# MLP, shared experts and router in an order written by hand on three engines, and slots' rows and gates loaded with their tokens

## The chip, the core and the metric

The kernel runs on one core of a Trainium2 chip. The metric is the device time of one execution in microseconds; the time before is the median of three runs. The core has a matrix engine (TensorE, PE in the profile), a vector engine (VectorE, DVE), a scalar engine (ScalarE, ACT), a general engine (GpSimd, POOL) and a synchronisation engine (SyncE, SP). Each works through its own list of instructions in order. Transfers between the chip's memory (HBM) and the on-chip buffers are issued from the lists of SyncE, ScalarE or GpSimd, and an issue that must wait holds what stands behind it in that list. A matmul writes to a bank of the accumulator memory, from which VectorE and ScalarE read.

## What is computed

One layer: 512 query rows of width 512 attend to 8192 context rows (16 heads), then a state-space block with a gated MLP, then a mixture of experts with top-2 routing and a shared expert. The reference, cut to what this change touches:

```python
x = x + _L0_xattn_ref(_layernorm(x), ctx, ctx, ...)          # cross attention
# state-space block and MLP, on the LayerNorm of x
z = layernorm(x)
z = z + _ssm(rmsnorm(z, norm1_w), ...)
h = rmsnorm(z, norm2_w)
mlp = (silu(h @ w1) * (h @ w3)) @ w2                          # D_FF = 2048
x = x + z + mlp
# experts, on the LayerNorm of x
t = layernorm(x)
logits = t @ router_w.T                                       # 16 experts
top_vals, top_idx = top_k(logits, 2)
gates = sigmoid(top_vals)
h_e = silu(t @ gate_e) * (t @ up_e)                           # EXPERT_DIM = 512
moe = sum over the two chosen experts of gate * (h_e @ down_e)
shared = (silu(t @ rsg.T) * (t @ rsu.T)) @ rsd.T              # SHARED_DIM = 1024
x = x + moe + shared
```

## The kernel before

Every f32 product is made of three f16 products (high times high, high times low, low times high), so a 128x128 by 256 block of the MLP costs three matmuls, and each f16 operand is a pair (high, low): ScalarE makes the high half by a cast or copy, VectorE the low half by a subtraction.

**Stages.** Attention over the context takes about the first two thirds. Then come the output projection, the state-space scan, the MLP, the LayerNorm `ln2`, the router, the shared experts and the experts. The 512 tokens are two halves s = 0, 1 of H = 256. The MLP of half 0 runs as filling inside the scan of half 1; the MLP of half 1, both halves of the shared experts and the router follow after the scan, and it is these that the change edits.

**`ffn` (L962-986)** is used for the MLP (weights w1, w3, w2; eight chunks f2) and for the shared experts (rsg, rsu, rsd; four chunks). For one chunk it loads three weight tiles `wpm` (ring of five slots, 512 KB each, from SyncE), runs 24 matmuls of 256 columns into the bank `pg` and 24 into `pu`, then g = silu(pg) on ScalarE (L973), g = pu * g on VectorE (L974), `gg` high half by a cast on ScalarE (L976), low half on VectorE (L977), and then 12 matmuls of 512 columns, `mm_down` (L716 to L718), into two accumulators. Banks pg, pu, and the banks of transposes and logits rotate over three. At its end the half's accumulators are added to `x_sb` (L985). It is a generator that yields once a chunk and is stepped by its callers.

**`ln2(s)` (L995-1019)** computes the statistics of x_sb (VectorE), a reciprocal root by Ln and Exp on ScalarE (L669, L670, each with a load of its activation table) and four small steps on VectorE, then the normalised tokens into `u_sb`, their transposes on TensorE, and the router's logits `plg` (24 small matmuls) copied to `lg`.

**Router (L1133-1215).** Tokens are written as f16 pairs to `xf`, whose rows have XR = 1028 16-bit words: 1024 for the pair, two for the token's row number, two for its gate. Then maxima and indices, sigmoid of the two best logits, ranks of tokens within experts by small matmuls (`prk`), slot numbers `sg` (L1191), and eight indirect DMAs from GpSimd (L1212), which scatter the rows to `xd_d` in HBM: four with the first gate, then, after a copy of the second gate into xf (L1210) that has to wait for the first four, four more. Slots are groups of 128 rows: one for each of the 16 experts and up to seven for overflow, two of which always run, so 18 slots k are processed. The overflow slots' expert numbers are put into `oii` (L1204), which SyncE reads into registers (L1342).

**Experts (L1217-1340).** `moe_load(k)` loads slot k with two DMAs that wait for all eight scatters: the token words `xd` from ScalarE's list (four buffers), and the last four words of the rows, `xm`, from GpSimd's list (eight buffers, 128 rows of 8 bytes). `moe_in` transposes xd to `xk`, `moe_up` makes 96 matmuls (banks pmg, pmu), `moe_mid` the activation, `moe_down` 12 matmuls, and `moe_out` scales with the gate on ScalarE (`myo`, L1284) and adds the rows to `sum_d` in HBM by an indirect, accumulating DMA from GpSimd (L1285). Each scatter-add waits for the one before it. Slots 0 to 2 are loaded ahead of the loop, slot k+3 within iteration k. Expert weights come as `piece`s of 512 KB (L1091-1106): a load into `wef` (six buffers, SyncE), a conversion to f16 on ScalarE (L1104) and its rest on VectorE (L1105). Twenty up-projection pieces (NWE) are made ahead of the experts.

**What sets the order.** All of this is written as source, but a scheduler places the instructions of each engine by its own costs, except within `manual_schedule`, where the named engines keep source order. Before, only the call of `moe` stands in such a block, with TensorE, VectorE and ScalarE named. So the twenty early pieces, which the source has last, are placed where the scheduler puts them: the profile has their conversions between 2249 and 2317. It also puts a part of each chunk's down matmuls inside the next chunk's gate block. SyncE's and GpSimd's lists are placed by the scheduler throughout. At the end the sum `sum_d` is started from x_sb by a DMA from GpSimd (L1347) and copied to the output (L1357).

## Time and profile before

| what | us |
|---|---|
| median of three runs | 2584.93 (2579.12 to 2588.01) |
| the profiled execution's own time | 2596.24 |
| its span, first to last instruction | 2594.4 |
| its mean granted TensorE clock | 0.973 of full speed |
| TensorE busy | 2376.9 (92%) |
| VectorE busy | 2045.9 (79%) |
| ScalarE busy | 1949.5 (75%) |
| GpSimd busy | 83.1 (3%) |
| first expert matmul (pmg) | 2407.5 |
| last scatter-add issued | 2581.8 |
| output copy issued | 2588.1 |

Times within the run are microseconds from the start of the span. In a listing by time a row is: start, duration, engine, line, operation, result <- operands, and in brackets the idle time of that engine before it and what ended it. In a list of waits a row is: engine, what waited and its line, what it waited for, the total in us, the number of times, and the longest. In a table of windows, each engine has its busy time and, in brackets, its number of instructions; the last three columns are the granted clock, the busy share of the DMA engines and the GB/s they moved. "L973" is line 973 of the kernel before. ACTq and SPq are the DMA issues of ScalarE and SyncE.

### The profile page before, as it was taken

What the parts mean: (1) busy time and instruction counts of PE and PEld (TensorE: products, weight loads), DVE (VectorE), ACT (ScalarE), POOL (GpSimd) and SP (SyncE); (2) the same over time, 40 slices, a digit from 0 to 9 for tenths busy, and PEclk for the clock granted to TensorE, in tenths of its full rate; (3) what the DMA queues carried; (4) which work ended last, traced back from release to release, by engine and by line L of the source; (5) the groups of instructions that cost most, each with busy time, mean ns of one, the idle gap of its engine ahead of it and who ended that gap; (6) DMA issues with size and microseconds to landing.
All of it is one profiled execution on the core that took longest, in us unless ns stands there. A gap on an engine that the chain in (4) does not pass through costs nothing. (4 is left out here: it accounts for less than half of the span.)

```text
span 2594.4 us, 56739 instructions
## 1 busy us (share of the span) xinstructions
PE 2376.9 (92%) x22958; PEld 1726.7 (67%) x22958; DVE 2045.9 (79%) x2378; ACT 1949.5 (75%) x3734; POOL 83.1 (3%) x92
## 2 busy tenths in 40 slices
PE   7999899999999999999999998998878687898996
PEld 3455577777677777666777776997656465665784
DVE  6776578888888888887888778997899999643684
ACT  5787788888788888878888887997868466432684
POOL 3000000000000000000000000000000000001122
PEclk9999999999999999999999999999989889999998
DMA  7883777788787787878787665888511222595796
GB/s 264 293 277 132 209 213 226 237 233 235 206 233 226 225 243 230 240 201 223 227 236 211 180 164 136 205 204 214 153 57 42 90 74 81 192 327 191 273 359 203
DMA packets 355967, 529.52 MB, mean 204 GB/s; under 512 B 28770, under 2 KB 222498, under 8 KB 355428
## 3 DMA queue, kind: packets, MB, share of 16 engines
q1 hardware_dynamic: 349156, 513.23, 65.7%
q0 software_dynamic: 3952, 7.89, 1.5%
q10 hardware_dynamic: 2592, 4.72, 0.5%
q8 instruction: 182, 2.98, 0.5%
q14 instruction: 85, 0.70, 0.1%
HBM read 396.65 MB, written 126.97 MB: 202 GB/s over the span
## 5 line engine op out<-in xcount | busy, mean ns | idle before, releaser
L380 DVE TENSOR_TENSOR phl<-p,phl 128x1024 f16<-128x1024 f32 x512 | 626.7, 1225 | 192.7 <-ACT phl L377 179.6
L375 ACT ACTIVATE p<-pss 128x512 f32<-128x512 f32 x1024 | 597.5, 622 | 113.6 <-issue 43.6
L308 ACT ACTIVATE sf<-psx 128x512 f16<-128x512 f32 x1024 | 558.7, 625 | 70.3 <-PE psx L303 69.5
L367 PE MATMUL pss<-qhh,k 128*128 128x256 f16 x2048 | 480.8, 275 | 11.2 <-ACT phl L377 10.3
L368 PE MATMUL pss<-qlm,kb 128*128 128x256 f16 x2048 | 479.0, 274 | 0.7 <-DMA kb<-k_d 0.5
L316 DVE TENSOR_TENSOR runm<-runm,sf 128x2048 f16<-128x2048 f16 x240 | 292.3, 1219 | 51.1 <-ACT sf L308 50.9
L397 PE MATMUL po<-v,phl 128*128 128x130 f16 x4096 | 323.7, 221 | 3.9 <-DVE oq L410 3.4
L377 ACT ACTIVATE phl<-pss 128x512 f16<-128x512 f32 x512 | 312.8, 611 | 0.0
L397 PEld LDWEIGHTS <-phl 128*128 128x128 f16 x4096 | 271.7, 98 | 61.7 <-issue 15.3
L278 PE MATMUL psv<-wh_v,ctxc 128*128 128x256 f16 x1024 | 283.4, 277 | 7.3 <-ACT wh_v L179 3.2
L279 PE MATMUL psv<-wl_v,ctxc 128*128 128x256 f16 x1024 | 282.2, 276 | 1.2 <-DVE wl_v L180 1.2
L280 PE MATMUL psv<-wh_v,ctxc 128*128 128x256 f16 x1024 | 282.0, 275 | 0.0
L367 PEld LDWEIGHTS <-k 128*128 128x128 f16 x2048 | 201.0, 98 | 64.7 <-issue 19.1
L368 PEld LDWEIGHTS <-kb 128*128 128x128 f16 x2048 | 201.3, 98 | 50.5 <-issue 12.7
L303 PE MATMUL psx<-khl,qh 64*128 64x512 f16 x1024 | 209.1, 386 | 18.7 <-ACT sf L308 13.2
L929 PE MATMUL py<-hs,ident 128*128 128x256 f32 x512 | 142.7, 434 | 74.0 <-DVE hs L926 73.9
L400 PE MATMUL po<-v,phl 128*128 128x65 f16 x4096 | 208.5, 193 | 1.3 <-DVE phl L380 1.2
L254 PE MATMUL psk<-ctxc,wh_k 128*128 128x512 f16 x512 | 197.9, 386 | 10.9 <-ACT ctxc L237 9.1
L379 DVE CAST phl<-p 128x1024 f16<-128x1024 f32 x256 | 176.1, 688 | 32.3 <-ACT p L375 32.1
L255 PE MATMUL psk<-ctxc,wh_k 128*128 128x512 f16 x512 | 196.3, 383 | 0.7 <-DVE ctxc L238 0.7
L256 PE MATMUL psk<-ctxc,wl_k 128*128 128x512 f16 x512 | 196.3, 383 | 0.0
L929 PEld LDWEIGHTS py<-hs,ident 128*128 128x128 f32 x512 | 106.0, 215 | 106.5 <-DVE hs L926 87.9
(308 smaller groups left out, 3834.8 us busy)
## 6 DMA issues: line engine op xcount, KB each, us to landing
v<-v_d SPq DMA_DIRECT2D x128, 520.0 KB, 5.3
k<-k_d SPq DMA_DIRECT2D x256, 256.0 KB, 4.7
ctxc<-ctx_d SPq DMA_DIRECT2D x96, 512.0 KB, 5.8
wef<-in_gu_dram SPq DMA_DIRECT2D x72, 512.0 KB, 6.8
v_d<-vs SPq DMA_DIRECT2D x128, 260.0 KB, 4.1
k_d<-khl SPq DMA_DIRECT2D x128, 256.0 KB, 3.0
kb<-k_d SPq DMA_DIRECT2D x128, 256.0 KB, 5.3
wpm<-w_d SPq DMA_DIRECT2D x48, 512.0 KB, 4.2
```

Of the source, the lines that this page charges most:

```text
L278: nc.tensor.matmul(ps[:, t, :], lhsT=ct[i // 2][:, 0, i % 2, sl], rhs=wh[:, i, :], start=i == 0, stop=False)
L279: nc.tensor.matmul(ps[:, t, :], lhsT=ct[i // 2][:, 0, i % 2, sl], rhs=wl[:, i, :], start=False, stop=False)
L280: nc.tensor.matmul(ps[:, t, :], lhsT=ct[i // 2][:, 1, i % 2, sl], rhs=wh[:, i, :], start=False, stop=i == NC4 - 1)
L308: nc.scalar.activation(dst, ps, AF.Copy, scale=1.0 / (8.0 * WS))
L316: nc.vector.tensor_tensor(r, r, sf, ALU.max)
L367: nc.tensor.matmul(ps[:, hh], lhsT=k[:, hh, sl], rhs=qhh[:, hh, qs], start=True, stop=False)
L368: nc.tensor.matmul(ps[:, hh], lhsT=b[:, hh, sl], rhs=qlm[:, hh, qs], start=False, stop=True)
L375: nc.scalar.activation(p32[:, i], pss[i], AF.Exp, scale=sc)
L377: nc.scalar.activation(ph[:, i], pss[i], AF.Exp, scale=sc)
L380: nc.vector.tensor_tensor(pl, p32, ph, ALU.subtract)
L397: nc.tensor.matmul(o, lhsT=ph[:, i, hh, qs], rhs=vv, start=first, stop=False, **kw)
L929: nc.tensor.matmul(py[:, j, :], lhsT=ident, rhs=hs[:, n, 1:], start=k == 0, stop=False)
```

## The change

1. `ffn_ordered` takes the place of `ffn` for the MLP of half 1 and for the shared experts. It writes a chunk as pg, pu with silu, the down matmuls of the chunk before, then g and gg, with three yields a chunk.
2. `ln2` becomes a generator, and the router's code moves into a generator `route`; their steps are interleaved with the chunks by counters.
3. The twenty early pieces are made one by one between the steps by `early` (nine in the MLP of half 1, five and six in the two halves of the shared experts).
4. The block in which TensorE, VectorE and ScalarE keep source order is opened ahead of `outproj(1)` and closed after `moe`.
5. The addition of u_sb to x_sb for half 1 moves out of `outproj` to after the rest of half 0's MLP.
6. `moe_load(k, queue)` loads the whole row of 1028 words by one DMA into `xd` (six buffers); row numbers and gates are read from it, and xm is gone. Slots 0 to 2 are loaded from GpSimd's list, later ones from ScalarE's.

```diff
@@ outproj
-        nc.vector.tensor_add(x_sb[:, ts_, :], x_sb[:, ts_, :], u_sb[:, ts_, :])
+        if not s:
+            nc.vector.tensor_add(x_sb[:, ts_, :], x_sb[:, ts_, :], u_sb[:, ts_, :])
...
+    def ffn_ordered(s, h2, names, pm):
...
+        prev = None
+        for f2 in range(nf):
+            wg, wu, wd = (wload(n, f2) for n in names)
+            pg = bank_j([P, 2, H], F32, "pg")
+            for j in range(2):
+                mm_block(pg[:, j, :], wg, j, h2[:, 0], h2[:, 1])
+            yield
+            pu = bank_j([P, 2, H], F32, "pu")
+            for j in range(2):
+                mm_block(pu[:, j, :], wu, j, h2[:, 0], h2[:, 1])
+            g = F2.tile([P, 2, H], F32, name="g32", bufs=2)
+            nc.scalar.activation(g, pg, AF.Silu, scale=IW)
+            yield
+            if prev:
+                down(*prev)
+            nc.vector.scalar_tensor_tensor(g, pu, IW, g, ALU.mult, ALU.mult)
+            gg = F2.tile([P, 2, 2, H], F16, name="gg", bufs=2)
+            nc.scalar.copy(gg[:, 0], g)
+            nc.vector.tensor_tensor(gg[:, 1], g, gg[:, 0], ALU.subtract)
+            yield
+            prev = f2, gg, wd
+        down(*prev)
+        yield
...
+    mo = ExitStack()
+    mo.enter_context(tc.manual_schedule(engines={mybir.EngineType.PE, mybir.EngineType.DVE, mybir.EngineType.Activation}))
     outproj(1, yTs[-1], h2s[1], lambda: next(ml, None))
     for _ in ml:
         pass
+    nc.vector.tensor_add(x_sb[:, 2:4, :], x_sb[:, 2:4, :], u_sb[:, 2:4, :])
...
+    mlp1 = ffn_ordered(1, h2s[1], MLP, [acc(0), acc(1)])
+    xT0, xT1 = h2tile(), None
+    l0 = ln2(0, xT0)
+    pre = iter(range(NWE))
+
+    def early():
+        n = next(pre, None)
+        if n is not None:
+            piece(n // 4, "gu", n % 4)
+
+    for n, _ in enumerate(mlp1):
+        if n in (0, 5, 7, 9):
+            next(l0, None)
+        if n % 3 == 1:
+            early()
+    xT1 = h2tile()
+    l1, ro = ln2(1, xT1), route()
+    rs0 = ffn_ordered(0, xT0, RS, [acc(3), acc(3)])
+    next(l1)
+    for n, _ in enumerate(rs0):
+        if n in (4, 5, 7):
+            next(l1, None)
+        elif n > 7:
+            next(ro, None)
+        if n % 3 == 1:
+            early()
+    for n, _ in enumerate(ffn_ordered(1, xT1, RS, [acc(3), acc(3)])):
+        next(ro, None)
+        early()
+    for _ in ro:
         pass
...
-    def moe_load(k):
+    def moe_load(k, queue):
         if k > lastk[0]:
             return
-        xds[k] = g2.tile([P, 2 * DM], U16, name="xd", bufs=4)
-        meta[k] = g2.tile([P, 4], U16, name="xm", bufs=8)
-        for q, t, c in ((nc.scalar, xds[k], slice(0, 2 * DM)), (nc.gpsimd, meta[k], slice(2 * DM, XR))):
-            r = q.dma_start(t, xd_d[k * P : (k + 1) * P, c])
+        xds[k] = g2.tile([P, XR], U16, name="xd", bufs=6)
+        r = queue.dma_start(xds[k], xd_d[k * P : (k + 1) * P, :])
...
         for k in range(ks[0], ks[0] + 3):
-            moe_load(k)
+            moe_load(k, nc.gpsimd)
...
-            moe_load(k + 3)
+            moe_load(k + 3, nc.scalar)
...
-    for _ in rs0:
-        pass
-    for _ in ffn(1, xT1, RS, [acc(3), acc(3)]):
-        pass
     nc.gpsimd.dma_start(sum_d[0:NQ].rearrange("(p i) d -> p i d", i=4), x_sb)
-    for n in range(NWE):
-        piece(n // 4, "gu", n % 4)
-    with tc.manual_schedule(engines={mybir.EngineType.PE, mybir.EngineType.DVE, mybir.EngineType.Activation}):
-        moe(range(16 + MOV), NWE)
+    moe(range(16 + MOV), NWE)
+    mo.close()
```

`route` holds the router's code of L1133 to L1215 in the same order, except that the computation of oii is moved behind the scatters, with seven yields between its parts: before the low half of xf, before the sigmoid, two before the rank matmuls (`prk`), one after them, one after the scatters and one at its end.

More of the change, by code (lines that the diff above doesn't have):

```diff
@@ L986, in ffn, with down @@
         yield
+    def ffn_ordered(s, h2, names, pm):
+        nf = len(mlp_d[names[0]])
+        def down(f2, gg, wd):
+            for i in range(2):
+                sl = slice(i * P, (i + 1) * P)
+                for j in range(2):
+                    k = 2 * f2 + j
+                    mm_down(pm[i], gg[:, 0, j, sl], gg[:, 1, j, sl], wd, j, k == 0, k == 2 * nf - 1)
+        prev = None
[6 more added lines that the diff above has]
+            pu = bank_j([P, 2, H], F32, "pu")
+            for j in range(2):
+                mm_block(pu[:, j, :], wu, j, h2[:, 0], h2[:, 1])
[12 more added lines that the diff above has]
+        yield
+        for i in range(2):
+            nc.vector.scalar_tensor_tensor(x_sb[:, 2 * s + i], pm[i], IW, x_sb[:, 2 * s + i], ALU.mult, ALU.add)
+        yield
     rwf = T.tile([P, NC4, 16], F32, name="rwf")
@@ L993, in tail, with ln2 @@
     lg = T.tile([P, 4, 16], F32, name="lg")
-    def ln2(s, xT, fill=lambda: None):
+    def ln2(s, xT):
         ts_ = slice(2 * s, 2 * s + 2)
@@ L1005, in ln2 @@
             )
-        fill()
+        yield
         transposeT(h, xT[:, 0], xT[:, 1])
-        fill()
+        yield
         pl = bank_j([P, 2, 16], F32, "plg")
@@ L1018, in ln2 @@
                     n += 1
+        yield
         nc.scalar.activation(lg[:, ts_, :], pl, AF.Copy, scale=IW)
+        yield
     MLP, RS = ("w1", "w3", "w2"), ("rsg", "rsu", "rsd")
@@ L1122, in tail @@
     nc.gpsimd.memset(one16, 1.0)
-    mlp1 = ffn(1, h2s[1], MLP, [acc(0), acc(1)])
-    next(mlp1)
-    xT0 = h2tile()
-    ln2(0, xT0, lambda: next(mlp1))
-    for _ in mlp1:
-        pass
-    xT1 = h2tile()
-    rs0 = ffn(0, xT0, RS, [acc(3), acc(3)])
-    ln2(1, xT1, lambda: next(rs0, None))
-    xf = const.tile([P, 4, XR], U16, name="xf", tag="big16")
-    xv = xf[:, :, 0 : 2 * DM].bitcast(F16)
-    nc.scalar.copy(xv[:, :, 0:DM], u_sb)
-    nc.vector.tensor_tensor(xv[:, :, DM : 2 * DM], u_sb, xv[:, :, 0:DM], ALU.subtract)
@@ L1137, in tail @@
-    nc.gpsimd.iota(xf[:, :, 2 * DM : 2 * DM + 2].bitcast(I32), pattern=[[1, 4], [0, 1]], base=0, channel_multiplier=4)
-    mx = G.tile([P, 4, 8], F32, name="mx8")
-    ix = G.tile([P, 4, 8], U32, name="ix8")
-    for i in range(4):
-        nc.vector.max(mx[:, i, :], lg[:, i, :])
-        nc.vector.max_index(ix[:, i, :], mx[:, i, :], lg[:, i, :])
-    ef = G.tile([P, 4, 2], F32, name="ef")
-    nc.vector.tensor_copy(ef, ix[:, :, 0:2])
-    gt = G.tile([P, 4, 2], F32, name="gt")
-    nc.scalar.activation(gt, mx[:, :, 0:2], AF.Sigmoid)
@@ L1148, in tail @@
-    oh = G.tile([P, 2, 4, 16], F32, name="oh")
-    iob = io16.unsqueeze(1).to_broadcast((P, 4, 16))
-    for j in range(2):
-        nc.vector.tensor_tensor(
-            oh[:, j], iob, ef[:, :, j : j + 1].to_broadcast((P, 4, 16)), ALU.is_equal
-        )
-    oht = G.tile([P, 4, 16], F16, name="oht")
-    nc.vector.tensor_add(oht, oh[:, 0], oh[:, 1])
-    next(rs0, None)
-    prk = bank_j([P, 5, 16], F32, "prk")
-    for i in range(5):
-        n = min(i, 4)
-        if i < 4:
-            nc.tensor.matmul(prk[:, i, :], lhsT=lt, rhs=oht[:, i, :], start=True, stop=n == 0)
-        for k in range(n):
-            nc.tensor.matmul(
-                prk[:, i, :], lhsT=ones, rhs=oht[:, k, :], start=i == 4 and k == 0, stop=k == n - 1
-            )
@@ L1166, in tail @@
-    rk = G.tile([P, 5, 16], F32, name="rk")
-    nc.vector.tensor_copy(rk, prk)
-    ov = G.tile([P, 16], F32, name="ov")
-    nc.vector.tensor_scalar(ov, rk[:, 4, :], 128.0, None, ALU.is_gt)
-    for th in (256.0, 384.0):
-        nc.vector.scalar_tensor_tensor(ov, rk[:, 4, :], th, ov, ALU.is_gt, ALU.add)
-    inc = G.tile([P, 16], F32, name="inc")
-    nc.vector.tensor_tensor_scan(inc, one16, ov, 0.0, ALU.mult, ALU.add)
-    ahi = G.tile([P, 16], F32, name="ahi")
-    nc.vector.tensor_sub(ahi, inc, ov)
@@ L1176, in tail @@
-    nc.vector.tensor_sub(ahi, ahi, io16)
-    nc.vector.tensor_scalar(ahi, ahi, 128.0, 15.0 * P, ALU.mult, ALU.add)
-    sl3 = G.tile([P, 4, 16], F32, name="sl3")
-    nc.vector.tensor_scalar(sl3, rk[:, 0:4, :], 128.0, None, ALU.is_ge)
-    nc.vector.tensor_mul(sl3, sl3, ahi.unsqueeze(1).to_broadcast((P, 4, 16)))
-    nc.vector.tensor_add(sl3, sl3, rk[:, 0:4, :])
-    e128 = G.tile([P, 16], F32, name="e128")
-    nc.vector.tensor_scalar(e128, io16, 128.0, None, ALU.mult)
-    nc.vector.tensor_add(sl3, sl3, e128.unsqueeze(1).to_broadcast((P, 4, 16)))
@@ L1185, in tail @@
-    sf_ = G.tile([P, 2, 4], F32, name="slf")
-    tmp = G.tile([P, 2, 4, 16], F32, name="tmp")
-    for j in range(2):
-        nc.vector.tensor_mul(tmp[:, j], oh[:, j], sl3)
-        nc.vector.tensor_reduce(sf_[:, j], tmp[:, j], axis=AX.X, op=ALU.add)
-    sg = G.tile([P, 2, 4], U32, name="sg")
-    nc.vector.tensor_copy(sg, sf_)
-    ct = G.tile([P, NOV, 16], F32, name="ct")
-    nc.vector.tensor_tensor(
-        ct,
-        inc.unsqueeze(1).to_broadcast((P, NOV, 16)),
-        io16[:, 0:NOV].unsqueeze(2).to_broadcast((P, NOV, 16)),
-        ALU.is_le,
-    )
@@ L1199, in tail @@
-    oid = G.tile([P, NOV + 1], F32, name="oid")
-    nc.vector.tensor_reduce(oid[:, 0:NOV], ct, axis=AX.X, op=ALU.add)
-    nc.vector.tensor_scalar(oid[:, 0:NOV], oid[:, 0:NOV], 15.0, None, ALU.min)
-    nc.vector.tensor_copy(oid[:, NOV : NOV + 1], inc[:, 15:16])
-    oii = G.tile([P, NOV + 1], I32, name="oii")
-    nc.vector.tensor_copy(oii, oid)
-    sent = []
-    gs = G.tile([P, 4, 2], F32, name="gs")
-    nc.vector.tensor_scalar(gs, gt, IW, None, ALU.mult)
-    for j in range(2):
-        nc.gpsimd.tensor_copy(xf[:, :, XR - 2 : XR].bitcast(F32), gs[:, :, j : j + 1])
-        for i in range(4):
-            d = nc.gpsimd.indirect_dma_start(
-                out=xd_d[:], out_offset=bass.IndirectOffsetOnAxis(ap=sg[:, j, i : i + 1], axis=0),
-                in_=xf[:, i], in_offset=None,
-            )
-            for o in sent:
-                tc.declare_no_dep(d.ins, o.ins, reason="every slot is one token's: the rows differ")
-            sent.append(d)
@@ L1220, in moe_load, with route @@
-    def moe_load(k):
+    oii = G.tile([P, NOV + 1], I32, name="oii")
+    sent = []
+    def route():
+        xf = const.tile([P, 4, XR], U16, name="xf", tag="big16")
+        xv = xf[:, :, 0 : 2 * DM].bitcast(F16)
+        nc.scalar.copy(xv[:, :, 0:DM], u_sb)
+        yield
+        nc.vector.tensor_tensor(xv[:, :, DM : 2 * DM], u_sb, xv[:, :, 0:DM], ALU.subtract)
+        nc.gpsimd.iota(xf[:, :, 2 * DM : 2 * DM + 2].bitcast(I32), pattern=[[1, 4], [0, 1]], base=0, channel_multiplier=4)
+        mx = G.tile([P, 4, 8], F32, name="mx8")
+        ix = G.tile([P, 4, 8], U32, name="ix8")
+        for i in range(4):
+            nc.vector.max(mx[:, i, :], lg[:, i, :])
+            nc.vector.max_index(ix[:, i, :], mx[:, i, :], lg[:, i, :])
+        ef = G.tile([P, 4, 2], F32, name="ef")
+        nc.vector.tensor_copy(ef, ix[:, :, 0:2])
+        gt = G.tile([P, 4, 2], F32, name="gt")
+        yield
+        nc.scalar.activation(gt, mx[:, :, 0:2], AF.Sigmoid)
+        oh = G.tile([P, 2, 4, 16], F32, name="oh")
+        iob = io16.unsqueeze(1).to_broadcast((P, 4, 16))
+        for j in range(2):
+            nc.vector.tensor_tensor(
+                oh[:, j], iob, ef[:, :, j : j + 1].to_broadcast((P, 4, 16)), ALU.is_equal
+            )
+        oht = G.tile([P, 4, 16], F16, name="oht")
+        nc.vector.tensor_add(oht, oh[:, 0], oh[:, 1])
+        yield
+        yield
+        prk = bank_j([P, 5, 16], F32, "prk")
+        for i in range(5):
+            n = min(i, 4)
+            if i < 4:
+                nc.tensor.matmul(prk[:, i, :], lhsT=lt, rhs=oht[:, i, :], start=True, stop=n == 0)
+            for k in range(n):
+                nc.tensor.matmul(
+                    prk[:, i, :], lhsT=ones, rhs=oht[:, k, :], start=i == 4 and k == 0, stop=k == n - 1
+                )
+        yield
+        rk = G.tile([P, 5, 16], F32, name="rk")
+        nc.vector.tensor_copy(rk, prk)
+        ov = G.tile([P, 16], F32, name="ov")
+        nc.vector.tensor_scalar(ov, rk[:, 4, :], 128.0, None, ALU.is_gt)
+        for th in (256.0, 384.0):
+            nc.vector.scalar_tensor_tensor(ov, rk[:, 4, :], th, ov, ALU.is_gt, ALU.add)
+        inc = G.tile([P, 16], F32, name="inc")
+        nc.vector.tensor_tensor_scan(inc, one16, ov, 0.0, ALU.mult, ALU.add)
+        ahi = G.tile([P, 16], F32, name="ahi")
+        nc.vector.tensor_sub(ahi, inc, ov)
+        nc.vector.tensor_sub(ahi, ahi, io16)
+        nc.vector.tensor_scalar(ahi, ahi, 128.0, 15.0 * P, ALU.mult, ALU.add)
+        sl3 = G.tile([P, 4, 16], F32, name="sl3")
+        nc.vector.tensor_scalar(sl3, rk[:, 0:4, :], 128.0, None, ALU.is_ge)
+        nc.vector.tensor_mul(sl3, sl3, ahi.unsqueeze(1).to_broadcast((P, 4, 16)))
+        nc.vector.tensor_add(sl3, sl3, rk[:, 0:4, :])
+        e128 = G.tile([P, 16], F32, name="e128")
+        nc.vector.tensor_scalar(e128, io16, 128.0, None, ALU.mult)
+        nc.vector.tensor_add(sl3, sl3, e128.unsqueeze(1).to_broadcast((P, 4, 16)))
+        sf_ = G.tile([P, 2, 4], F32, name="slf")
+        tmp = G.tile([P, 2, 4, 16], F32, name="tmp")
+        for j in range(2):
+            nc.vector.tensor_mul(tmp[:, j], oh[:, j], sl3)
+            nc.vector.tensor_reduce(sf_[:, j], tmp[:, j], axis=AX.X, op=ALU.add)
+        sg = G.tile([P, 2, 4], U32, name="sg")
+        nc.vector.tensor_copy(sg, sf_)
+        gs = G.tile([P, 4, 2], F32, name="gs")
+        nc.vector.tensor_scalar(gs, gt, IW, None, ALU.mult)
+        for j in range(2):
+            nc.gpsimd.tensor_copy(xf[:, :, XR - 2 : XR].bitcast(F32), gs[:, :, j : j + 1])
+            for i in range(4):
+                d = nc.gpsimd.indirect_dma_start(
+                    out=xd_d[:], out_offset=bass.IndirectOffsetOnAxis(ap=sg[:, j, i : i + 1], axis=0),
+                    in_=xf[:, i], in_offset=None,
+                )
+                for o in sent:
+                    tc.declare_no_dep(d.ins, o.ins, reason="every slot is one token's: the rows differ")
+                sent.append(d)
+        yield
+        ct = G.tile([P, NOV, 16], F32, name="ct")
+        nc.vector.tensor_tensor(
+            ct,
+            inc.unsqueeze(1).to_broadcast((P, NOV, 16)),
+            io16[:, 0:NOV].unsqueeze(2).to_broadcast((P, NOV, 16)),
+            ALU.is_le,
+        )
+        oid = G.tile([P, NOV + 1], F32, name="oid")
+        nc.vector.tensor_reduce(oid[:, 0:NOV], ct, axis=AX.X, op=ALU.add)
+        nc.vector.tensor_scalar(oid[:, 0:NOV], oid[:, 0:NOV], 15.0, None, ALU.min)
+        nc.vector.tensor_copy(oid[:, NOV : NOV + 1], inc[:, 15:16])
+        nc.vector.tensor_copy(oii, oid)
+        yield
@@ L1225, in moe_load @@
-        for q, t, c in ((nc.scalar, xds[k], slice(0, 2 * DM)), (nc.gpsimd, meta[k], slice(2 * DM, XR))):
-            r = q.dma_start(t, xd_d[k * P : (k + 1) * P, c])
-            for o in sent:
-                tc.add_manual_dep(
-                    r.ins, o.ins.name, mybir.DependencyInfo(mybir.DependencyClass.Sync, mybir.DependencyReason.DATA),
-                    reason="rows of every scatter",
-                )
-    xds, meta, lastk = {}, {}, [0]
+        xds[k] = g2.tile([P, XR], U16, name="xd", bufs=6)
@@ L1235, in moe_in @@
+        r = queue.dma_start(xds[k], xd_d[k * P : (k + 1) * P, :])
+        for o in sent:
+            tc.add_manual_dep(
+                r.ins, o.ins.name, mybir.DependencyInfo(mybir.DependencyClass.Sync, mybir.DependencyReason.DATA),
+                reason="rows of every scatter",
+            )
+    xds, lastk = {}, [0]
     def moe_in(k):
-        xd, m = xds.pop(k), meta.pop(k)
+        xd = xds.pop(k)
         pt = bank_j([P, 2, NC4, P], F16, "pxd")
@@ L1243, in moe_in @@
         xk = g2.tile([P, 2, NC4, P], F16, name="xk", bufs=2)
-        return xk, pt, m[:, 0:2].bitcast(U32), m[:, 2:4].bitcast(F32)
+        return xk, pt, xd[:, 2 * DM : 2 * DM + 2].bitcast(U32), xd[:, 2 * DM + 2 : XR].bitcast(F32)
     def moe_up(k, xk):
@@ L1342, in tail @@
     regs = [nc.sync.value_load(oii[0:1, k : k + 1], min_val=0, max_val=15) for k in range(NOV)]
-    for _ in rs0:
-        pass
-    for _ in ffn(1, xT1, RS, [acc(3), acc(3)]):
-        pass
     nc.gpsimd.dma_start(sum_d[0:NQ].rearrange("(p i) d -> p i d", i=4), x_sb)
-    for n in range(NWE):
-        piece(n // 4, "gu", n % 4)
-    with tc.manual_schedule(engines={mybir.EngineType.PE, mybir.EngineType.DVE, mybir.EngineType.Activation}):
-        moe(range(16 + MOV), NWE)
+    assert next(pre, None) is None
+    moe(range(16 + MOV), NWE)
+    mo.close()
     total = nc.values_load(oii[0:1, NOV : NOV + 1], min_val=0, max_val=NOV)
```

## The prediction

> **What bounds it now.** I read the whole run by slices first, then the stage that the change edits by windows, by waits and by time.

> ```profile
> PE   7999899999999999999999998998878687898996
> PEclk9999999999999999999999999999989889999998
> ```

> TensorE is the bound almost everywhere, and the edited stage holds two of the slices with a lower digit. The windows give that stage (PE and its count, then the other engines, granted clock, DMA share, GB/s):

> ```profile
> 2250.00:2260.00 10.00, 6.87 (x39) 3.90 (x38) 7.63 (x14) 6.52 (x10) 0.00 (x0) 0.83 0.83 302
> 2260.00:2330.00 70.00, 65.36 (x511) 47.02 (x509) 36.43 (x53) 29.92 (x39) 0.00 (x0) 1.00 0.92 324
> 2330.00:2340.00 10.00, 7.66 (x59) 5.48 (x57) 5.61 (x14) 7.42 (x10) 0.00 (x0) 1.00 0.63 235
> 2370.00:2380.00 10.00, 1.71 (x15) 1.19 (x13) 0.69 (x1) 0.57 (x1) 5.52 (x8) 0.79 0.70 259
> 2380.00:2390.00 10.00, 9.89 (x52) 5.95 (x53) 0.96 (x2) 0.65 (x2) 2.84 (x6) 0.70 0.48 158
> 2407.00:2571.00 164.00, 155.99 (x2092) 126.60 (x2091) 128.16 (x126) 131.95 (x160) 37.61 (x27) 1.00 0.92 316
> ```

> Two stretches stand out, 2250–2260 and 2370–2390: idle first, then matmuls at a lower clock. The waits of TensorE from 2228 to 2412 say for whom:

> ```profile
> PE acc L716 <- ACT gg L976: 14.6, 7, 7.7
> PE pg L710 <- DVE g L974: 3.1, 2, 2.3
> PE pg L710 <- DMA wpm<-rsg_d: 0.7, 1, 0.7
> PE pmg L1255 <- ACT xk L1312: 1.1, 1, 1.1
> ```

> The down projection waits for the cast of gg on ScalarE. The longest wait, by time on ScalarE and GpSimd:

> ```profile
> 2378.08 1.31 ACTq L1226 DMA_DIRECT2D xd<-xd_d  x3
> 2379.43 0.62 ACT L976 CAST gg<-g 128x512 f16<-128x512 f32 x1 [11.24 <-issue]
> 2370.35 0.19 POOL L1210 COPY xf<-gs 128x4 f32<-128x4 f32 x1 [6.15 <-DMA xd_d<-xf,sg]
> 2378.53 3.78 POOL L1226 DMA_DIRECT2D xm<-xd_d  x7 [2.74 <-DMA xd_d<-xf,sg]
> ```

> ScalarE's issue slot holds three xd loads that need the last router scatter; the cast of gg stands behind them, and TensorE stood from 2372.37 to 2380.11. Afterwards, in the experts, GpSimd's pattern and the chain that ends last:

> ```profile
> 2480.16 0.58 POOL L1226 DMA_DIRECT2D xm<-xd_d  x1 [6.84 <-DMA sum_d<-myo,xm]
> 2481.04 2.08 POOL L1285 DMA_INDIRECT sum_d<-myo,xm  x1 [0.31 <-ACT mg L1263]
> 2576.45 1.55 DMA sum_d<-myo,xm
> 2578.00 3.64 issue
> 2582.13 1.27 POOL sum_d L1285
> ```

> The scatter-adds end the run: ScalarE's last myo ends at 2570.6, the last scatter-add starts at 2581.84, 11.2 later.

> **The sum for TensorE.** From 2250.29 (last transpose of h) to the experts' first own matmul. That one starts at 2407.53, with 12 down matmuls (216 ns apart, 2.6) mixed in, so I count to 2410.1: 159.8 us. Work: 48 matmuls of 256 columns at 109 ns (5.23) and 12 at 216 ns (2.59) make 7.82 a chunk; 16 chunks 125.1; the last down of the first half 2.6; transposes 2 x 1.1, router logits 2 x 1.55, ranks 0.8, xd transposes 0.6. Together 134.4. The ten gaps over 0.25 us (3.12, 0.56, 0.73, 1.18, 1.07, 0.77, 2.34, 0.67, 7.74, 1.10) make 19.3. The remaining 6.1 is the clock: 39 and 52 matmuls in the windows at 0.83 and 0.70, some 75 in one at 1.00.

> *In source order.* Down(f) now follows pu(f+1), so gg has 7.8 us (down, pg, pu) from the end of pu(f), and needs g, cast and difference, about 2. The early pieces come one by one (nine in the MLP, five and six in the shared halves); each puts 1.05 on ScalarE and 1.22 on VectorE in front of something, with some 5.8 us of slack for gg. I laid the new instruction order out by hand with the durations of before (g and gg's low half 0.69, cast and silu 0.6, table load 1.28, LayerNorm steps as they stood). These stalls of TensorE are left, each an estimate from those rows: 1.3 at the start (the cast 0.6 after g, low half 0.7 later; no longer behind the piece that came at 2251.79, which waited 1.50 for its load); 2.1 in the first MLP chunks (a silu behind the two table loads of the first rsqrt holds a bank, 0.6, and the first gg, 1.4); 1.5 in the first shared half (the second rsqrt's table loads and four small VectorE steps, in three places); 1.0 before its last down (copy into xf and sigmoid's table load ahead of gg's cast); 0.5 entering the second half (piece and rank arithmetic ahead of g); 1.3 for xk (1.10 before). Sum 7.6; bounds 0 (all fall under the slack) and 16 (each twice as long). The longest is 1.4, and the 2.34 gap before 2336 left the clock at 1.00, so I take no clock loss; one 3 us stall brings back some 2 to 4.
> Gain: 19.3 + 6.1 − 7.6 = **17.8**, bounds 9 and 25.

> [...]

> *Weight loads.* With five wpm slots, each load is released about three blocks (7.8 us) before use and lands in 3.3 to 6.3. Demand: three loads of 524,288 bytes a 7.82 us chunk, plus one piece, is 268 GB/s; in the second shared half (six pieces) 302; both below the 324 drawn here. Before, 20 pieces fell in 2249–2317, and chunks at 2273–2295 took about 10 us. Against a late landing I hold back **2.0** (two of the three gaps of 0.73 to 1.18 there). The register reads on SyncE stand before a late shared load; that load has 5 us to spare.

> *Moved x_sb addition (L957):* 1.21 us of VectorE, from the chain h takes to TensorE to where down matmuls cover it; uncovered it costs 1.2, and where it stood it saves at most as much; cost 0.

> *Router.* It is now spread over steps; by the schedule the MLP ends at 2321.4 (2250.3 + 1.3 + 2.6 + 62.6 + 2.6 + 2.1), the first shared half's last pu 30.3 later at 2351.7 (four pairs 20.9, two downs 5.2, transposes and logits 2.7, stalls 1.5), its last down and the ranks at 2358.7 (5.2 + 1.0 + 0.8); sg follows the ranks by 4.0 as before: 2362.7, against 2358.3 before. Scatter, copy and scatter again by the rows of before (0.9, 11.16, 8.18) put the xd loads, on GpSimd now, at 2382.9; issue 0.55 (the x_sb load of that queue), landing 2.8 (xm) to 5.3 (ScalarE's xd): 2386.2 to 2388.8. TensorE wants xd at 2390.5 (31.3 and 0.5 for the second half). Cover 1.7 to 4.3, cost 0; if it fails, 1:1, and ScalarE's gg no longer waits there. Behind these loads on GpSimd: sum_d<-x_sb (0.55), needed only by the first scatter-add 20 us on.
> [...]

> *New wait.* xd(k+3) on ScalarE has six slots and waits for scatter-add k−3. Behind it stand xk(k+1), for which TensorE waits, and mgg. Slack 3.8 us at k = 3, 0.3 less each expert: never used if scatter-adds come 9.1 apart. Cost 0; upper bound, TensorE at the scatters' pace, which then ends the run anyway: loss of the tail gain below.

> *Tail.* Between scatter-adds in 2430–2520 the mean is 9.96, including an xm load (0.57 and 0.30 of issue). Without it 9.1, against 8.81 an expert on TensorE: 0.28 x 14 = 4 of lag, in place of (9.96 − 8.81) x 9, about 10. The last scatter-add comes **5.2** nearer to the last myo. Bounds: 0 (landing under load sets the pace) and 11.2 (no lag left).

> **Sum:** −17.8 + 2.0 − 5.2 = −21.0. The profiled execution took 2596.24 (span 2594.4), 11.3 above the median 2584.93 (2579.12 to 2588.01); I apply the difference to the median: **2564**.

> **Rivals.**
> *Gain half lost at GpSimd:* the tail stays (0) and the second scatter group takes as long as the first (11.16, +3.0), xd lands in 7.6 as late pieces do (+2.3): 5.3 less 1.7 of cover, 3.6, and 4 of clock. −17.8 + 2 + 7.6 = −8.2: 2577. For it: GpSimd's 70 us of waits for landings. Against: DMA share falls after 2340.
> *Stalls only move:* in-order ScalarE and VectorE give back 19.3 + 6.1 elsewhere; only the tail counts: 2580. For it: 20 pieces waited 19.2 us for wef. Against: loads run six pieces ahead, 47 us at one a chunk.
> *Slower, DMA saturated through the stage:* every chunk at the 10 us of 2273–2295, 16 x 2.2 = 35, no stalls besides, one clock loss 6, tail −5: 159.8 becomes 134.4 + 35 + 6 = 175.4, net +10.6: 2595. It decides from about 1.6 us lost a chunk (25.4/16). For it: 0.92 share, and in-order queues pass any late load on. Against: 268 to 302 GB/s asked.
> *That it doesn't do what it says:* the built order has it on three engines; SyncE and GpSimd are still scheduled.

> **How the numbers follow.** Forecast 0.60, own range 2552 to 2573 (stall, tail bounds). Half lost 0.14, moved 0.12, slower 0.14. 0.3% is 7.8 us, about what a measurement can tell: faster means below 2577. Half-lost gives 0.08 faster, 0.06 same; moved 0.04 and 0.08; slower 0.13, 0.01 same. Faster 0.72, same 0.15, slower 0.13. Range 2551 (stalls near 0, tail near full) to 2584.

> **What would show it.** First pmg matmul near 2392; no TensorE gap over 1.5 from 2250 to there, clock 1.00; gg's cast behind no DMA; xd landed before TensorE ends the shared half; scatter-adds about 9.1 apart, the last near 2559; span about 2573. Wrong if chunks last beyond 9 us, if TensorE waits for xd, or if ScalarE's xd issue waits in the experts.

## The result, and the profile after

| | before | changed |
|---|---|---|
| median, us (7 runs each) | 2588.01 (2579.12 to 2594.81) | 2568.02 (2565.43 to 2574.79) |
| ratio | | 0.9926, 95% interval 0.9912 to 0.9940 |
| profiled span, us | 2594.4 | 2563.7 |

The change makes the kernel 20.0 us faster by the medians; the interval of the ratio is 15.5 to 22.8 us. The forecast was 21.0 less than before.

The two profiled executions differ by more, 30.7 us. Cut into stretches (us from the start of each span):

| stretch | before | changed | difference |
|---|---|---|---|
| start to TensorE's last transpose of h | 2250.3 | 2243.1 | −7.2 |
| from there to the experts' first matmul | 159.8 (to 2410.1, as the prediction counts) | 139.7 (to 2382.8) | −20.1 |
| first expert matmul to last myo | 159.8 | 163.5 | +3.7 |
| last myo to last scatter-add | 11.9 | 5.1 | −6.8 |
| last scatter-add to the end | 12.6 | 12.3 | −0.3 |

The first stretch has the same instruction order on TensorE, VectorE and ScalarE in both, up to the end of the scan. The last VectorE product of the scan (L926) starts at 2223.7 before and 2216.4 after, and between 2216.4 and 2222.6 in the profiles of the twelve experiments below: this part of the difference is the execution, not the change. The other four rows sum to −23.5, which is some 0.7 us more than the interval of the medians allows; a single pair of profiles is not better than that, and the shares below are read with this in mind. The profiled execution of the kernel before took 2596.24 us, longer than any of its seven timed ones; that of the changed kernel, 2565.43, is the shortest of its seven.

The waits of TensorE in the edited stage of the changed kernel, from 2243 to 2383 (total us, times, longest):

```profile
PE pxd L1315 <- DMA xd<-xd_d: 2.2, 1, 2.2
PE acc L716 <- ACT gg L1017: 1.2, 2, 0.7
PE pmg L1328 <- ACT xk L1385: 1.1, 1, 1.1
PE acc L716 <- ACT gg L977: 0.6, 1, 0.6
PE pu L710 <- ACT g L1011: 0.6, 1, 0.6
PE pt L693 <- ACT g L1011: 0.4, 1, 0.4
```

The cast of gg, 14.6 us of waits before, is down to 1.8. A wait that was not there before leads the list: the first slot's xd. The windows of the same stage show the rest:

```profile
2260.00:2320.00 60.00, 60.00 (x481) 45.23 (x479) 24.67 (x37) 20.40 (x30) 0.00 (x0) 1.00 0.79 269
...
2360.00:2380.00 20.00, 18.88 (x135) 13.02 (x133) 9.02 (x12) 5.57 (x8) 7.13 (x9) 1.00 0.99 360
2380.00:2400.00 20.00, 16.64 (x232) 14.88 (x233) 10.67 (x11) 11.17 (x13) 0.45 (x1) 0.91 0.67 234
```

TensorE is busy in all of 2260–2320, at full clock, with 269 GB/s as summed in the prediction (268). In 2360–2380 the transfers are at 0.99 of the DMA engines; that is when the router's second scatters are under way. After the wait for xd the clock is at 0.91. GpSimd by time, and the chain that ends last:

```profile
2369.19 0.96 POOL L1240 DMA_INDIRECT xd_d<-xf,sg  x1 [0.30 <-issue]
2377.71 1.68 POOL L1300 DMA_DIRECT2D xd<-xd_d  x3 [7.56 <-DMA xd_d<-xf,sg]
...
2472.88 1.55 POOL L1358 DMA_INDIRECT sum_d<-myo,xd  x1 [7.26 <-issue]
2482.26 1.55 POOL L1358 DMA_INDIRECT sum_d<-myo,xd  x1 [7.83 <-issue]
```

```profile
2545.94 1.55 DMA sum_d<-myo,xd
2547.49 3.74 issue
...
2551.72 1.26 POOL sum_d L1358
```

The last scatter took 7.56 us to land where it took 2.74 before. Between scatter-adds there is no xm load any more; the end is still the chain of scatter-adds, but it starts 5.1 behind the last myo.

Last, what ScalarE waited for in the experts (2390 to 2560), one line of that view:

```profile
ACT xk L1401 <- DMA sum_d<-myo,xd: 6.3, 5, 2.0
```

Five times a slot load on ScalarE's list waited for an earlier scatter-add, with the copy xk behind it. Before, this line does not exist.

### The profile page after: what moved, and what is told of

The parts are those of the page before. It is cut to its first block, busy times and chain, and to the rows that moved or that the text cites. A ratio compares the mean times of both kernels' runs of the same rounds, so it can differ in the third digit from the quotient of the medians.

```text
span 2563.7 us, 56681 instructions
## 1 busy us (share of the span) xinstructions
PE 2361.3 (92%) x22958; PEld 1722.3 (67%) x22958; DVE 2046.2 (80%) x2378; ACT 1947.5 (76%) x3734; POOL 73.8 (3%) x77
## 5 line engine op out<-in xcount | busy, mean ns | idle before, releaser
L367 PE MATMUL pss<-qhh,k 128*128 128x256 f16 x2048 | 478.3, 274 | 14.1 <-ACT phl L377 11.9
```

What stands on the lines that cost most here:

```text
L367: nc.tensor.matmul(ps[:, hh], lhsT=k[:, hh, sl], rhs=qhh[:, hh, qs], start=True, stop=False)
```

## The experiments

Every kernel was timed beside the kernel before on the same chip; medians of the runs of each, and the ratio to before. "Against changed" is the difference to 2568.0; the changed kernel was not timed beside them, and by the ratios some of these differences change sign (a_early_sooner and a_two_xf then both lie 1.3 below it).

| run | median, us | ratio to before (95%) | against changed |
|---|---|---|---|
| b_first3_gpsimd | 2579.66 | 0.9964 (0.9949–0.9979) | +11.6 |
| b_whole_rows | 2576.86 | 0.9951 (0.9933–0.9970) | +8.8 |
| b_rows_down_later | 2569.53 | 0.9929 (0.9905–0.9954) | +1.5 |
| a_scheduler | 2568.50 | 0.9921 (0.9902–0.9939) | +0.5 |
| a_early_two | 2568.22 | 0.9922 (0.9904–0.9939) | +0.2 |
| a_down_at_once | 2616.27 | 1.0113 (1.0087–1.0139) | +48.2 |
| a_rows_apart | 2569.06 | 0.9924 (0.9900–0.9949) | +1.0 |
| a_first3_scalar | 2568.32 | 0.9925 (0.9901–0.9949) | +0.3 |
| a_early_sooner | 2569.76 | 0.9921 (0.9906–0.9936) | +1.7 |
| a_two_xf | 2567.33 | 0.9921 (0.9904–0.9938) | −0.7 |
| a_xk_sooner | 2575.81 | 0.9949 (0.9935–0.9963) | +7.8 |
| a_xk_early | 2571.40 | 0.9932 (0.9919–0.9946) | +3.4 |

With four to seven runs each, the 95% interval of a difference between two of these kernels reaches 3 to 5 us either way, so differences under some 4 us are not told apart.

### From the kernel before, one part at a time

**b_first3_gpsimd**

```diff
-        for q, t, c in ((nc.scalar, xds[k], slice(0, 2 * DM)),
+        for q, t, c in ((nc.gpsimd if k < 3 else nc.scalar, xds[k], slice(0, 2 * DM)),
```

> The kernel before, with one edit: the loads of xd for slots 0 to 2 are issued from GpSimd's list and not from ScalarE's. Theory A (the 7.74 us gap is ScalarE's cast of gg standing behind these loads, and the low clock after it comes with the gap): the gap at gg is gone, the clock stays at 1.00, 10 to 12 us less than before; the tail stays (scatter-adds 10 apart under load). Rival B (this block is all that the change cures): about 20 us less. Rival C (the xd loads end the wait in either place, only the hand-written order helps): within 3 us of before.

Measured: 9.9 us less than before. TensorE's waits in the stage:

```profile
PE acc L716 <- ACT gg L976: 5.9, 6, 2.6
PE pg L710 <- DVE g L974: 3.1, 2, 2.3
```

The 7.7 us entry is gone, the others stay. Theory A holds for this block; it is half of the change's gain, and neither all of it (B) nor none (C). Its last part fails: the tail did not stay. Here the first fourteen scatter-adds are 9.27 apart (9.78 before) and the last starts 6.8 behind the last myo (11.9 before), with the xm loads still between them. From the landing of one scatter-add to the start of the next takes 1.17 with an xm load between them and 0.72 without, before and here alike, so such a load costs 0.45 us; the landings themselves, 6.9 to 10.2 us in this profile's first fourteen, vary by more than that.

**b_whole_rows**

```diff
-        xds[k] = g2.tile([P, 2 * DM], U16, name="xd", bufs=4)
-        meta[k] = g2.tile([P, 4], U16, name="xm", bufs=8)
...
+        xds[k] = g2.tile([P, XR], U16, name="xd", bufs=6)
+        queue = nc.gpsimd if k < 3 else nc.scalar
+        r = queue.dma_start(xds[k], xd_d[k * P : (k + 1) * P, :])
```

> The kernel before, with the change's slot loads alone: whole rows by one DMA, six buffers, the first three from GpSimd; router, shared experts and MLP as the scheduler had them. Theory A: as with the first three loads moved, and 3 to 5 us more from the end, as scatter-adds come 9.1 to 9.4 apart: 13 to 16 us less than before. Rival B: about 20 less. Rival C: 0 to 5 less, from the tail alone.

Measured: 12.7 us less than before, 2.8 less than the run above (intervals overlap). All of the change's slot loads together are 12.7 of 20.

**b_rows_down_later**: the same, with the down matmuls of a chunk written behind the next chunk's pu. Router, early pieces and scheduler stay as before.

```diff
+            nc.scalar.activation(g, pg, AF.Silu, scale=IW)
+            if prev:
+                down(*prev)
+            nc.vector.scalar_tensor_tensor(g, pu, IW, g, ALU.mult, ALU.mult)
...
-    mlp1 = ffn(1, h2s[1], MLP, [acc(0), acc(1)])
+    mlp1 = ffn_ordered(1, h2s[1], MLP, [acc(0), acc(1)])
```

> The kernel before with whole rows and, in the MLP and the shared experts after the scan, the down matmuls of a chunk written behind the next chunk's pu; all engines still ordered by the scheduler, router and early pieces in their old place. Theory E (the later down is what ends the gaps at gg, neither the pinned order nor the interleaving of router and pieces): the gaps at gg under 1 us except perhaps the first, 18 to 22 us less than before, within 2 us of the changed kernel. Theory A (pinned order and interleaving): as whole rows alone, 11 to 14 us less than before.

Measured: 19.7 us less than before. With this one edit on top of the slot loads the changed kernel's time is reached, without its pinned order and without its interleaving. The view of waits:

```profile
PE acc L716 <- ACT gg L976: 2.3, 1, 2.3
PE pmg L1289 <- ACT xk L1346: 1.1, 1, 1.1
PE pg L710 <- DMA wpm<-rsg_d: 1.0, 1, 1.0
```

One wait for gg is left of seven: the last chunk of the first half's MLP, which this edit doesn't touch. Theory A, that pinning and interleaving carry this share, falls.

### From the changed kernel, one part undone

**a_scheduler**

```diff
-    mo = ExitStack()
-    mo.enter_context(tc.manual_schedule(engines={...}))
     outproj(1, yTs[-1], h2s[1], lambda: next(ml, None))
...
+    with tc.manual_schedule(engines={...}):
+        moe(range(16 + MOV), NWE)
```

> The changed kernel, with the block of source order opened only around the experts, as before; the new source stays. Theory A (the order on the engines is worth the gaps other than the 7.74: 11.5 and 2 of clock less 7.6 new stalls): the scheduler puts conversions early and in front of casts again, 5 to 9 us more than the changed kernel. Rival B: within 2 us of the changed kernel.

Measured: no difference (+0.5); expected 5 to 9 more. The scheduler keeps the source's later down matmuls, but puts the early pieces where it likes, close together. Its windows, and two conversions on ScalarE:

```profile
2280.00:2300.00 20.00, 20.00 (x159) 15.39 (x158) 9.85 (x10) 9.91 (x12) 0.00 (x0) 1.00 0.96 351
2300.00:2320.00 20.00, 20.00 (x141) 13.70 (x140) 9.60 (x12) 7.45 (x10) 0.00 (x0) 1.00 0.98 354
```

```profile
2288.16 1.06 ACT L1146 ACTIVATE we<-wef 128x1024 f16<-128x1024 f32 x1 [0.98 <-DMA wef<-in_gu_dram]
...
2293.04 1.06 ACT L1146 ACTIVATE we<-wef 128x1024 f16<-128x1024 f32 x1 [3.24 <-DMA wef<-in_gu_dram]
```

ScalarE still waits for late pieces, up to 3.24 us, at 351 to 354 GB/s, more than the 324 of before; and TensorE is busy in every microsecond of these windows. The late pieces were not cured: gg now has the slack to bear them.

**a_early_two**

```diff
         if n % 3 == 1:
             early()
+            early()
```

> The changed kernel, with two early pieces a chunk in the MLP (18 there, 2 in the first shared half). Theory A (a gg has some 5.8 us of slack, so two conversions a chunk still fit, and the demand of 335 GB/s is just above the 324 that were drawn): 1 to 4 us more than the changed kernel. Rival D (DMA traffic in this stage decides): chunks of 10 us, 10 us or more above the changed kernel.

Measured: +0.2, told apart neither from none nor from theory A's 1 to 4. One gap grew (1.81 us at the first gg, with half the clock granted from 2263.20 to 2266.61, which is the 0.91 of 2260–2280 in this run); the 2.2 us wait for xd went, as nothing is loaded for pieces in the second shared half. Rival D, chunks of 10 us when transfers crowd, falls here (TensorE busy for 39.75 of the 40 us of 2280–2320, at 0.89 and 0.93 of the DMA engines) and in the run above (40.00, at 0.96 and 0.98).

**a_down_at_once**

```diff
-            if prev:
-                down(*prev)
...
+            down(f2, gg, wd)
             yield
```

> The changed kernel, with a chunk's down matmuls directly behind its own gg in the source of ffn_ordered, order still pinned. Theory E: TensorE waits in each of 16 chunks for g, cast and difference, about 1.5 to 2.3 us, 24 to 37 us more than the changed kernel, slower than before. Theory A (the pinned order itself helps): within 5 us of the changed kernel.

Measured: 48.2 more than the changed kernel, 1.1% slower than before. One line of the waits:

```profile
PE acc L716 <- ACT gg L1015: 41.1, 16, 6.7
```

All 16 chunks wait; most for 1.5 to 1.7 us, five of them for 3.1 to 6.7 where LayerNorm or router steps or an early piece stand ahead of g, so that the sum passes the 24 to 37 expected. From the last transpose of h to the first expert matmul the kernel takes 50.6 us more. Gaps over 0.25 us are 42.8 against 6.1, which is 36.7 of it. Half the clock was granted in four stretches of 6.83 us (from 2257.36, 2342.69, 2359.76 and 2397.30), in which TensorE was busy for 19.3 us: that is another 9.6, against none in this stage of the changed kernel. The remaining 4.3 stay open. Pinned order by itself is no gain: it makes a badly placed down certain.

**a_rows_apart**: xm is loaded apart again, from GpSimd's list; xd keeps six buffers.

```diff
+        xds[k] = g2.tile([P, 2 * DM], U16, name="xd", bufs=6)
+        meta[k] = g2.tile([P, 4], U16, name="xm", bufs=8)
+        for q, t, c in ((queue, xds[k], slice(0, 2 * DM)), (nc.gpsimd, meta[k], slice(2 * DM, XR))):
```

> The changed kernel, with row numbers and gates loaded apart again (xm from GpSimd's list; xd as it is, six buffers). The prediction's tail (0.87 us of GpSimd for each scatter-add under load): scatter-adds 10 apart, the last one 3 to 6 us further from the last myo, 3 to 5 us more than the changed kernel. Rival (landing of the adds sets the pace): no change within 1 us.

Measured: +1.0, not told apart from none. GpSimd by time:

```profile
2484.75 0.57 POOL L1302 DMA_DIRECT2D xm<-xd_d  x1 [7.23 <-DMA sum_d<-myo,xm]
2485.63 1.60 POOL L1360 DMA_INDIRECT sum_d<-myo,xm  x1 [0.30 <-ACT wpm L1148]
```

The first fourteen scatter-adds are 9.79 apart (9.39 in the changed kernel) and the last starts 9.4 behind the last myo (5.1), 4.3 worse in this pair of profiles. ScalarE never waits for a scatter-add here: an xd without the gates is free as soon as it is transposed, while the merged row holds its buffer until its scatter-add has read row numbers and gates. It would be a reason for the missing 4.3 if these waits had a cost, but that is not shown: from the first expert matmul to the last myo this run takes 164.6 us, the changed kernel with its 6.3 us of waits 163.5 (2.8 and 1.4 of these are half clock). The two profiled executions differ by 5.6 us, the medians by 1.0; why is open.

**a_first3_scalar**

```diff
-            moe_load(k, nc.gpsimd)
+            moe_load(k, nc.scalar)
```

> The changed kernel, with the first three slot loads on ScalarE's list. Theory A and E alike: in source order they stand behind the last gg, so nothing of the shared experts waits for them, and the queue does not matter: within 2 us of the changed kernel. Rival B (GpSimd's queue is what matters): 10 us more.

Measured: +0.3, not told apart from none. Once the order is pinned the queue of the first loads is of no account that can be seen; the 9.9 us of b_first3_gpsimd are what it cost where the scheduler put them ahead of a cast.

### Attempts to beat both

**a_early_sooner**

```diff
         if n % 3 == 1:
             early()
+            if n > 6:
+                early()
```

> The changed kernel, with the early pieces one a chunk in the first three MLP chunks and then two, four in the first shared half, none in the second. If TensorE's 2.2 us wait for the first slot comes from transfers that crowd the scatters (0.99 of the DMA engines busy then): the second scatters land within 4 us in place of 7.6, the wait is gone and the clock stays at 1.00; 2 to 4 us less than the changed kernel. Otherwise no change.

**a_two_xf**

```diff
+        xff = const.tile([P, 2, 4, XR], U16, name="xf", tag="big16")
+        xf = xff[:, 0]
...
+        nc.gpsimd.dma_start(xff[:, 1, :, 0 : XR - 2], xf[:, :, 0 : XR - 2])
...
-                    in_=xf[:, i], in_offset=None,
+                    in_=xff[:, j, i], in_offset=None,
```

> The changed kernel, with the rows of the second gate scattered from a copy of xf (made by one more DMA on GpSimd's list ahead of the gates), so that the second gate's copy waits for no scatter. The eight scatters go out 1.3 apart, the slot loads some 6 us sooner; TensorE's wait for the first slot is gone: 2 to 4 us less than the changed kernel. If landing under load decides alone, the slot loads still come about where they were: no change.

In a_early_sooner the edit makes two pieces from the third chunk on, not from the fourth: n is 7 there. GpSimd by time in the two runs:

```profile
2379.93 1.68 POOL L1302 DMA_DIRECT2D xd<-xd_d  x3 [5.55 <-DMA xd_d<-xf,sg]
```

```profile
2374.64 1.70 POOL L1302 DMA_DIRECT2D xd<-xd_d  x3 [6.13 <-DMA xd_d<-xf,sg]
```

In both profiles TensorE's wait for xd is gone and the clock stays at 1.00 there. In a_early_sooner the last scatter lands after 5.55 us (expected: within 4), with 0.78 of the DMA engines busy in 2360–2380; in a_two_xf after 6.13, with 1.00 busy, but the eight scatters go out in a row and the slot loads 7.3 us sooner in the stage. The times don't tell: +1.7 and −0.7. That the late slot loads cause the wait is shown; the 2 to 4 us are not seen in the medians. Part of them was lost again in the profiles: in both the clock falls later, in the experts (0.97 in 2400–2450, against 1.00 in the changed kernel).

**a_xk_sooner**

```diff
+            nxt = moe_in(k + 1) if k < last else None
+            if nxt:
+                nc.scalar.copy(nxt[0], nxt[1])
             piece(k, "dn", 1)
             n = split(each)
...
-            if k < last:
-                xin_ = moe_in(k + 1)
             next(mid)
```

> The changed kernel, with the transposes of slot k+1 and their copy xk one step sooner, ahead of the up-projection of slot k. In the profile of the changed kernel TensorE waits 8 us in the experts for xk on ScalarE, behind conversions that wait for their loads. If these waits set the pace: up to 7 us less than the changed kernel. If the expert weights' transfers do (0.96 of the DMA engines busy): TensorE waits for weights in their place, within 2 us.

Measured: 7.8 more than the changed kernel, against both expectations. TensorE no longer waits for xk, nor for weights, but 16 times for VectorE (12.3 us). VectorE by time:

```profile
2475.48 3.49 DVE L1149 SCALAR_TENSOR_TENSOR we<-wef,we 128x1024 f16<-128x1024 f32 x3
2478.89 0.68 DVE L1337 SCALAR_TENSOR_TENSOR mg<-pmu,mg 128x512 f32<-128x512 f32 x1
```

Three conversions in a row now stand ahead of mg, which frees the bank pmu of the next expert: 0.75 us lost an expert, 9.30 in place of 8.96 between two myo. Fifteen of the eighteen scatter-adds start 0.9 behind their myo (up to 7.8 behind in the changed kernel): at this pace they keep up.

**a_xk_early**: both edits.

> The changed kernel with both: xk one step sooner and the early pieces sooner. The sum of the two singles: up to 9 us less than the changed kernel, if weights' transfers do not set the pace; otherwise as the early pieces alone.

Measured: +3.4, with the same waits for mg. No version tried beats the changed kernel clearly.

## Why the prediction was right

The time (2564 forecast, 2568.0 measured) and the sign came from the place that the forecast named first, the gaps at gg. That the number is so close is partly luck. TensorE gained 20.1, against 15.8 in the forecast (17.8 less the 2.0 held back for weights), and the end brought less than its 5.2: no run shows it clear of noise. Also, two of its three "wrong if" signs came true: TensorE waited for xd (2.2), and ScalarE's xd issue waited in the experts (6.3).

*TensorE's sum.* 17.8 was forecast, 20.1 stands in the profiles. The work, 134.4, plus the seven gaps over 0.25 us (0.63, 0.58, 0.68, 0.44, 0.52, then 2.18 and 1.10 at the first slot: 6.1) gives 140.5 against 139.7 measured. The stalls summed to 7.6 in the forecast. Most were smaller than laid out (0.6 for 1.3 at the start, 1.3 for 2.1 in the first chunks, about 1.0 for 3.0 in the shared halves), and one was missing. What the forecast calls the clock, 6.1, is what was left over; by the records half the clock was granted before from 2252.97 to 2256.39 and from 2375.85 to 2386.09, with TensorE busy for 9.0 us in these, which is 4.5. The forecast took no clock loss since a gap of 2.34 had left the clock at 1.00; by the records that gap lay across two windows of 3.41 us, in which TensorE was busy for 1.84 and 2.64 (last section), and 2.18 at the first slot did cost some.

*The router's cover.* This is the term that was mis-sized: "Cover 1.7 to 4.3, cost 0". The xd loads were issued 134.6 us into the stage, against 132.6 forecast, and TensorE wanted them at 135.8, not at 140.2. The landing of the last scatter was taken from the row of before, 2.74, at a DMA share of 0.7; with six early pieces in the second shared half and experts' loads running ahead, the share was 0.99 and the landing 7.56. From the second copy into xf to the slot loads it took 14.1, not 8.18; only because sg and the first group came 3.9 sooner than forecast were the loads a mere 2.0 late. The forecast's rival "half lost at GpSimd" had the long second group (at 11.16), but not the rest of its 3.6: it had xd land in 7.6, and TensorE had the first xd 3.4 after its issue. The wait cost 2.2, and some 1.3 of clock (the first expert's matmuls and the next transposes took 7.3 against 6.0 in a_two_xf).

*In source order.* The mechanism named, down(f) behind pu(f+1) and 5.8 us of slack for gg, is the one that b_rows_down_later and a_down_at_once show from both sides. But the forecast did not separate it from the pinned order and the spread of the pieces, and those two are worth nothing measurable here (a_scheduler, a_early_two). The 2.0 held back for late weights was not needed in this stage.

*The tail.* −5.2 was forecast, and the numbers given for it (a lag of about 10, then 4) differ by 6. In the pair of profiles −6.8 came at the lag and +3.7 went in the experts, −3.1 together; in the medians whole rows are worth 2.8 (b_whole_rows against b_first3_gpsimd) and 1.0 (a_rows_apart), neither clear of noise. So this term was over-sized: it took 0.87 us for an xm load, which costs 0.45, and it took the lag of one execution (11.2 from the end of the last myo, 11.9 from its start) for that of the kernel, where b_first3_gpsimd, with the same xm loads, has 6.8 from the start. The new wait, "never used if scatter-adds come 9.1 apart", was used: they came 9.39 apart, the lag passed the slack of 3.8 from the fourth slot on, and ScalarE waited 6.3 us in the profile. That this has a cost is not shown: a_early_sooner has 7.1 us of such waits and takes 161.3 from the first expert matmul to the last myo, a_rows_apart has none and takes 164.6. Of the 3.7, some 1.3 is the half clock in the first expert; TensorE's waits for xk inside the experts rose by 1.5, from 5.5 to 7.0, and the rest is open.

*The rivals.* "Stalls only move" and "DMA saturated" are refuted, the second by windows at 354 GB/s without a gap. What had made the chunks of before 10 us long was gg's short lead over its down matmuls, not the transfers themselves.

## What to carry to other kernels

When matmuls consume what two other engines have to prepare, place them one block of matmuls later, and try this before an order is pinned by hand: here that edit brought the gain from 12.7 us (b_whole_rows) to 19.7 (b_rows_down_later) with the scheduler's order, and in a_scheduler TensorE was busy in all of 2280–2320 while ScalarE waited up to 3.24 us for a late piece. Before a transfer is merged with another, ask how long its buffer will then be held, and what stands behind the next load of that buffer; here that brought 6.3 us of waits, whose cost no run shows. Do not take a landing time read from a quiet stretch as a bound for the same transfer once more loads are moved into it: the router's last scatter landed in 2.74 us at 0.70 of the DMA engines before, and in 7.56 at 0.99 in the changed kernel.

## What the runs showed of the hardware that was not expected

The clock did not follow the length of a single idle stretch. One of 2.34 us left it at 1.00 (before, ending at 2335.66), while 2.18 and 1.10 with 0.6 of work between them brought it down to 0.50 (changed), and so did a single 1.81 (a_early_two). The records of the granted clock in the traces of these runs show what differed. Every stretch at 0.50, 27 of them before and 20 in the changed kernel, begins on a grid of 3.41 us, and all but the last, which runs to the end of the records, end on it: most last 3.41, the others 6.83 or 10.24. Below are the windows of that grid in which TensorE stood idle: two of before, one of the changed kernel with the window behind it, and one of a_early_two (TensorE's busy time comes first, the clock third from the end):

```profile
2249.56:2252.97 3.41, 0.73 (x7) 0.49 (x5) 1.97 (x3) 1.91 (x3) 0.00 (x0) 1.00 0.97 383
2331.48:2334.89 3.41, 1.84 (x17) 1.49 (x16) 0.50 (x4) 2.90 (x4) 0.00 (x0) 1.00 0.94 351
```

```profile
2378.70:2382.11 3.41, 0.80 (x9) 0.50 (x9) 1.82 (x2) 0.39 (x1) 1.24 (x3) 1.00 0.88 338
2382.11:2385.52 3.41, 2.74 (x27) 2.74 (x27) 1.23 (x1) 1.58 (x2) 0.00 (x0) 0.50 0.99 368
```

```profile
2259.79:2263.20 3.41, 1.47 (x11) 0.66 (x9) 2.58 (x4) 1.49 (x3) 0.00 (x0) 1.00 0.82 279
```
